# A two-layer graph network on one core: plain transfers grouped into fewer, larger ones

## The chip, the core and the metric

The kernel runs on one core of one Trainium2 chip. The core has a matrix engine (TensorE, PE in the profile; its weight loads are listed apart as PEld), VectorE (DVE), ScalarE (ACT), GpSimd (POOL) and SyncE (SP), and 16 DMA engines that move data between DRAM and the on-chip memory. SP does nothing but issue plain transfers; POOL computes a little and issues the indexed ones (a gather or a scatter whose row numbers come from a tile) and a few plain ones. The metric is the device time of one execution in microseconds.

## The reference

`x` is 2708 x 512 in float32, `adj` is 2708 x 2708 with a full diagonal and about 0.3% of the other entries set, to values between 0.05 and 1. Two layers follow each other, each with a residual and a layer norm:

```python
# layer 0
rowsum = adj.sum(axis=1)
d = jnp.where(rowsum > 0, rowsum ** (-0.5), 0.0)
g = relu(((d[:, None] * adj * d[None, :]) @ x) @ W + b)
x = layernorm(x + g)
# layer 1, 4 heads
y = x @ W_node + b_node
feats = jnp.einsum('nd,hdf->hnf', y, K)
s = leaky(einsum('hnf,hf->hn', feats, A_self) + einsum('hnf,hf->hn', feats, A_neigh))
attn = softmax(s[:, :, None] - 1e10 * (1.0 - adj)[None], axis=-1)
x = layernorm(x + relu(mean over h of (attn @ feats)))
```

In layer 1 the term with 1e10 leaves nothing of the softmax but a row's largest adj entry, so each row takes the features of one other row; and since the heads are averaged, `W_node` and the mean of `K` fold into one 512 x 512 matrix M (`m_sb`) with one bias row (`c_3`, `c_bc`).

## The kernel before

The 2708 rows are cut into 22 blocks of 128 rows (`NB`; the last has 20 rows, `NS` = 21 are full). All order is written by hand (`tc.manual_schedule()`): every engine and every queue works through its instructions in the order in which the program names them, and an instruction waits where it needs another engine's result or a buffer that is still in use. Pools with `bufs=n` give n buffers per name in turn; the writer of a buffer waits for the last reader of its previous content.

**Stage 1, to about 137 us.** For each block, SP loads its 1.35 MB of adj rows into one of nine slots (`a`, `load_blocks`, L289) and its rows of x (L525). PE turns x and multiplies it by W; ACT sums the adj rows (L296); POOL clears the diagonal (L307) and takes the root of the row sum (`root`, L262). `value` (L536) scales the product, giving v = d (x W), and stores it to `v_d` in DRAM: on POOL's queue for all but the last three blocks. DVE searches each adj row in three column thirds for its eight largest entries and their columns (`find`, L315). Blocks that the search has not reached by the end of stage 1 are searched later, between other work.

**Stage 2, to about 405 us.** A row has some eight neighbours. For each block, nine gathers fetch rows of `v_d` (`fetch_chunk`, L624, issued at L611): three "direct" ones (the first found column of each third), six from lists of what is left. The lists are made by `hot` (L385: for each third a `past` and a `hot` on DVE), `enlist` (a one-hot product on PE) and `listed` (L410, on DVE: `nth`, `one`, `own_f`, `sheet` and the lists). The fetched rows are summed by PE (`add_chunk`, L657 and L672, with small matrices that ACT or DVE forms) or by DVE (L662). Block `ib` also needs its own rows of v and of x: `load_own(ib + 2)` (L680, called at L1239) loads them two blocks ahead, on SP, into `vs` and `xr`. `norm_1` and the lines after it give h, the output of layer 0, in the tiles `h_early` (the first eight blocks) and `h_late`; each block of h is stored to `h_d` (L1188). Then `turn_h`, `u_product` and `u_store` (L772 to L798) give u = h M + c, stored to `u_e` (rows of the first `EARLY` = 18 blocks) or put by index into `u_d` (the rest). At L1232 to L1235 four stores, one for each of the blocks 9 to 12, fill the last block of `u_e` and `u_d` with finite values.

**Listed rows.** Rows that the search does not cover (over eight entries in a third, and the 20 rows of the last block) are listed once the search is done (`rank_1` to `rank_4`). Their rows of adj are gathered whole into `l_a` (`listed_a`, L981), and the full product with v is made: 22 turns (`listed_turn`) and 22 products (`listed_product`, L1008) on PE, against blocks of v that `listed_v` (L995) loads on SP into six buffers, `l_v`, six blocks ahead. When these steps come is written in `plan` (L1129), counted in blocks and chunks from the block at which the search ends.

**Stage 3, the output, from about 400 us.** For each block, `y_fetch` (L1042) gathers for each row the row of u of its largest neighbour, `y_1` (L1061) adds it to h, `root_1` and `root_2` (L739, L745) make the scale of the layer norm for a group of blocks, `y_3` applies it and the block is stored to `out`. The table `early_y` (L1073 to L1081) lays these steps out in pieces, in groups of three blocks. Rows whose largest neighbour is among the last blocks of u ("late" rows, at most four tiles) and the listed rows come last (L1256 to L1300) and are put into `out` by index; these puts wait for the plain stores of `out`. At the end a number from `bad` tells whether the sparse method covered the input; if not, a dense version runs instead (L1305), which it does not here.

Of the kernel before, what the change touches and what calls it, by code (L numbers as in the profile page):

```python
# [63 lines left out]
def tile_two_graph_layers(  # L64
# [36 lines left out]
    def store(dst, t, ib, queue=None):  # L101
        for lo, hi, r0 in parts(ib):
            (queue or nc.sync).dma_start(out=dst[r0 + lo : r0 + hi, :], in_=t[lo:hi])

    in_order = ExitStack()
# [279 lines left out]
    def hot(ib):  # L385

        lo = max(g for g in GROUPS if g <= ib)
        ends = starts[lo]
        h_t = search.tile([P, T, 2 * P], BF16, name="hot", bufs=2)
        for t in range(T):  # L390
            past = search.tile([P, 2 * P], BF16, name="past", bufs=2)
            nc.vector.tensor_scalar(past, slots, ends[:, 1, ib - lo, t : t + 1], None, op0=ALU.is_gt)  # L392
            nc.vector.scalar_tensor_tensor(  # L393
                h_t[:, t, :], slots, ends[:, 0, ib - lo, t : t + 1], past, op0=ALU.is_gt, op1=ALU.subtract
            )
        hots[ib] = h_t
# [13 lines left out]
    def listed(ib):  # L410

        ls = sheets.pop(ib)[:, : NL * W_REC].rearrange("p (n c) -> p n c", c=W_REC)
        nth = search.tile([P, NL], F32, name="nth", bufs=2)
        nc.vector.tensor_sub(nth, slot_no.rearrange("p t k -> p (t k)"), ls[:, :, 1])
        minus_row = search.tile([P, NL], F32, name="l_row", bufs=6)
        nc.vector.tensor_copy(minus_row, ls[:, :, 0])
        one = search.tile([P, NL, REST], F32, name="one", bufs=2)
        nc.vector.tensor_tensor(
# [5 lines left out]
        shape = [P, NL, 5, REST]  # L424
        own_f = search.tile(shape, F32, name="own_f", bufs=2)
        nc.vector.tensor_tensor(
# [4 lines left out]
        )  # L431
        t = search.tile([P, NL, 5], F32, name="sheet", bufs=2)
        nc.vector.tensor_reduce(t, own_f, axis=AX.X, op=ALU.add)
# [100 lines left out]
    pos_w = {}  # L534

    def value(i):  # L536

        pr = rows(i)
        vt = pool2.tile([P, D], F32, name=("vs", "xr")[i % 2], bufs=2)
        nc.scalar.activation(vt[:pr], pos_w.pop(i)[:pr], AF.Copy, scale=dinv[:pr, i : i + 1])  # L540
        store(v_d, vt, i, nc.gpsimd if i < NB - 3 else nc.sync)
        if i == 0:
            nc.gpsimd.dma_start(out=u_d[full - EARLY * P :, :], in_=vt[: N - full])
# [136 lines left out]
    def load_own(ib):  # L680
        if ib < NS:
            vs = pool2.tile([P, D], F32, name="vs", bufs=2)
            xr = pool2.tile([P, D], F32, name="xr", bufs=2)
            load(vs, v_d, ib)
            load(xr, x, ib)
            own[ib] = vs, xr

# [77 lines left out]
    def space(ib):  # L765
        if ib not in h_of:
            h_of[ib] = h_early[:, ib, :] if ib < NE else h_late[:, ib - NE, :]
        return h_of[ib]

    hTs = {}  # L770

# [5 lines left out]
    def u_product(ib):  # L777
        pr = P if ib == L else rows(ib)
        on_pe = searching[0]
        products_u[ib] = times(hTs.pop(ib), pr, m_sb, c_3 if on_pe else None), on_pe  # L780

    def u_store(ib):

        pr = P if ib == L else rows(ib)
        ut = dl["u"] if ib == L else pool2.tile([P, D], F32, name="ut", bufs=2)
        po, on_pe = products_u.pop(ib)
# [4 lines left out]
        if ib < EARLY - 1:  # L791
            store(u_e, ut, ib)
        elif ib == EARLY - 1:
            later(1, lambda: put(ut, u_e[:, :], dl["own"][:, ib : ib + 1], EARLY * P))
        elif ib != L:
            late_put = lambda: put(ut, u_d[:, :], dl["own_d"][:, ib : ib + 1], N - EARLY * P)
            late_put() if ib >= NS - 2 else later(3, late_put)
# [193 lines left out]
    def listed_root():  # L991
        dl["d"] = late.tile([P, 1], F32, name="l_d")
        root(dl["d"], dl["s2"])

    def listed_v(jb):  # L995
        if jb < NB:
            t = dl["v", jb] = late.tile([P, D], F32, name="l_v", bufs=6)
            load(t, v_d, jb)

# [8 lines left out]
    def listed_product(jb):  # L1008
# [5 lines left out]
        )  # L1014
        listed_v(jb + 6)
        if jb == NB - 1:
# [53 lines left out]

    GROUP = 3
    n_pieces = NS + 13
    early_y = [[] for _ in range(n_pieces)]  # L1073
    for n in range(NS):
        last = n // GROUP * GROUP + GROUP - 1
        early_y[n].append(lambda n=n: y_fetch(n))
        early_y[n + 6].append(lambda n=n: y_1(n))
        if n == last:
            early_y[last + 8].append(lambda n=n: root_1(n - GROUP + 1, n + 1))
            early_y[last + 9].append(lambda n=n: root_2(n - GROUP + 1, n + 1))  # L1080
        early_y[last + 10 + n % GROUP].append(lambda n=n: (y_3(n), store(out, h_of[n], n)))  # L1081

# [63 lines left out]
    for ib in range(NS):  # L1146
        pr = rows(ib)
        for c in range(C):
# [31 lines left out]
            if c == (2 if ib <= ROOTS_AT else 3) and ib:  # L1180
# [6 lines left out]
                norm_3(ib - 1, rows(ib - 1), space(ib - 1))  # L1187
                store(h_d, space(ib - 1), ib - 1)  # L1188
                waiting_h.append(ib - 1)
# [31 lines left out]
        if not finds and late is None:  # L1221
# [9 lines left out]
            nc.scalar.copy(c_bc, po)  # L1231
        at = ib - 10 + EARLY  # L1232
        if EARLY - 1 <= at < NS:

            store(*((u_e, space(ib - 9), at) if at < EARLY else (u_d, space(ib - 9), at - EARLY)))  # L1235
        if ib + 1 < NS:
# [12 lines left out]
    norm_v(ib, P, space(ib))  # L1249
    store(h_d, space(ib), ib)  # L1250
    stir(16)
# [44 lines left out]
    root_2(second[0], second[-1] + 1)  # L1296
    nc.vector.tensor_copy(bad_i, po[:1, :1])
    for n in second:
# [148 lines left out]
```

## Time and profile before

| | us |
|---|---|
| median of 3 runs | 490.34 (489.5 to 492.23) |
| profiled execution, its own time | 488.01 |
| its span in the trace | 486.3 |

Busy time by stretch of the span, in us, from the trace's table of time windows (PEclk is the granted clock of TensorE as a share of full speed, DMA the mean busy share of the 16 DMA engines):

| stretch (us) | length | PE | DVE | ACT | POOL | PEclk | DMA | GB/s |
|---|---|---|---|---|---|---|---|---|
| 0 to 115 | 115 | 90.99 | 95.07 | 94.35 | 49.72 | 0.93 | 1.01 | 367 |
| 115 to 137 | 22 | 21.02 | 18.67 | 19.18 | 11.20 | 0.98 | 0.54 | 200 |
| 137 to 270 | 133 | 113.20 | 128.49 | 84.55 | 100.11 | 0.97 | 0.81 | 256 |
| 270 to 310 | 40 | 29.57 | 31.18 | 22.89 | 28.60 | 0.88 | 0.91 | 311 |
| 310 to 400 | 90 | 88.82 | 65.81 | 48.33 | 65.70 | 0.98 | 0.92 | 323 |
| 400 to 414 | 14 | 13.59 | 10.66 | 4.50 | 8.02 | 1.00 | 0.80 | 258 |
| 414 to 486 | 72 | 19.64 | 41.85 | 38.51 | 41.99 | 0.68 | 0.63 | 208 |

The plain transfers that the change regroups, from the profile's list of DMA issues (number, KB of each, median us from issue to landing where the trace shows the landing): v stores on POOL's queue 10 `v_d<-vs` (7.3 us) and 9 `v_d<-xr` (7.5), `vs` 21 (4.9), `xr` 21 (5.9), `l_v` 21 (5.0), `u_e<-ut` 17, `h_d` 8 and 13 (3.6 and 2.9), `out_dram` 8 and 13 (4.8 and 4.4), all of 256 KB.

How to read the rest: a line of the timeline has a start in us, a duration in us, the engine (SPq and POOLq are issues on the queues of SP and POOL), the line of the code, the operation, and the tile written and the tiles read; in brackets stands the idle time before it and what ended that. Lines of the chain give shares of the span, followed back from the last instruction.

### The profile page before, as it was taken

The page shows a single profiled execution, that of the slowest core. Times are in us where ns is not written, and L with a number is a line of the kernel's source. Part 1 is how long each engine was busy: PE and PEld are TensorE (multiplying, and loading weights), DVE is VectorE, ACT ScalarE, POOL GpSimd, SP SyncE. Part 2 cuts the span into 40 slices and gives each one's busy share as a digit, 9 for nine tenths or more (in the row PEclk, how much of TensorE's full clock was granted, in tenths as well). Part 3 has the DMA queues.
Part 4 walks back from the last instruction along what each step waited for, and adds up shares of the span by engine and source line. Part 5 has one row for each costly group of instructions (what it writes and reads, how often), then busy time and mean ns, then how long its engine had stood idle before and what let it go on. Part 6 is the DMA issues. An engine that isn't in the chain of part 4 may idle for free.

```text
span 486.3 us, 5318 instructions
## 1 busy us (share of the span) xinstructions
PE 376.8 (77%) x1129; PEld 168.8 (35%) x1129; DVE 391.7 (81%) x1079; ACT 312.3 (64%) x575; POOL 305.3 (63%) x434
## 2 busy tenths in 40 slices
PE   4979788788978987799977958699999999880000
PEld 3434344333223333344323423344444444340000
DVE  2799989879799999999999996666667697667661
ACT  1599999797886556776773453865666322348680
POOL 2343544454477677777787577777777665677703
PEclk9998998798997999999999889799999999995555
DMA  7999999998548678889889789999999688469952
GB/s 232 419 398 416 422 339 371 357 336 342 197 119 286 202 235 264 263 253 315 272 258 290 228 261 371 376 325 376 369 367 313 219 270 269 138 194 308 322 193 84
DMA packets 51565, 140.67 MB, mean 289 GB/s; under 512 B 10617, under 2 KB 10617, under 8 KB 48688
## 3 DMA queue, kind: packets, MB, share of 16 engines
q0 software_dynamic: 21840, 68.29, 45.1%
q1 hardware_dynamic: 29684, 71.95, 39.4%
q8 instruction: 11, 0.18, 0.2%
q14 instruction: 30, 0.25, 0.2%
HBM read 117.33 MB, written 24.99 MB: 293 GB/s over the span
## 4 chain that ended last, share of the span: by engine, by line
DVE 28%; PE 19%; DMA 7%; issue 5%; ACT 3%; POOL 3%; POOLq 0%; DVEq 0%; ACTq 0%
PE acc L672 7%; PE po L235 6%; PE acc_l L1012 4%; DVE ats L319 4%; DVE vals L318 3%; DVE hot L393 3%; DVE vs L662 2%; DMA l_a<-in_adj_dram,to_read 2%; DMA g<-u_e,idx 2%; POOL g L611 1%; DVE past L392 1%; DVE h_early L712 1%; DMA g<-v_d,l_col 1%; DVE h_late L1063 1%; DVE vs L711 1%
## 5 line engine op out<-in xcount | busy, mean ns | idle before, releaser
L611 POOL DMA_INDIRECT g<-v_d,l_col x126 | 127.3, 1010 | 42.6 <-issue 22.1
L672 PE MATMUL acc<-g,s 128*128 128x512 f32 x278 | 143.2, 628 | 4.3 <-DMA g<-v_d,l_col 2.6
L235 PE MATMUL acc<-w_sb,sT 128*128 128x512 f32 (+1 forms) x176 | 89.1, 654 | 0.0
L235 PE MATMUL po<-m_sb,sT 128*128 128x512 f32 x176 | 80.8, 603 | 2.7 <-ACT sT L226 2.7
L611 POOL DMA_INDIRECT g<-v_d,cols x63 | 63.4, 1007 | 19.7 <-issue 13.1
L318 DVE MAX8 vals<-a 128x8 f32<-128x896 f32 (+2 forms) x66 | 71.7, 1087 | 2.8 <-ACT a L299 2.8
L319 DVE FIND_INDEX8 ats<-vals,a 128x8 uint32<-128x896 f32 (+2 forms) x66 | 72.1, 1092 | 0.0
L672 PEld LDWEIGHTS acc<-g,s 128*128 128x128 f32 x278 | 49.1, 196 | 50.1 <-issue 42.3
L305 ACT ACTIVATE a<-a 128x2708 f32<-128x2708 f32 (+1 forms) x22 | 54.4, 2471 | 12.4 <-DVE ats L319 12.4
L299 ACT ACTIVATE a<-a 128x2708 f32<-128x2708 f32 (+1 forms) x22 | 54.8, 2490 | 10.0 <-POOL a L311 10.0
L235 PEld LDWEIGHTS po<-m_sb,sT 128*128 128x128 f32 x176 | 33.5, 194 | 45.0 <-issue 38.2
L235 PEld LDWEIGHTS acc<-w_sb,sT 128*128 128x128 f32 (+1 forms) x176 | 34.7, 208 | 38.6 <-issue 38.5
L649 ACT ACTIVATE s<-s,l_val,l_minus 128x128 f32<-128x128 f32 x86 | 42.4, 493 | 2.9
L311 POOL TENSOR_SCALAR_AFFINE_SELECT a<-a 128x128 f32<-128x128 f32 (+1 forms) x22 | 7.2, 327 | 56.0 <-DMA a<-in_adj_dram 49.7
L226 ACT COPY sT<-tp 128x512 f32<-128x512 f32 (+1 forms) x44 | 25.8, 586 | 24.8 <-PE tp L224 24.8
L662 DVE SCALAR_TENSOR_TENSOR vs<-g,scaled,vs 128x512 f32<-128x512 f32 x50 | 37.2, 744 | 0.1
L224 PE MATMUL tp<-ident,x 128*128 128x128 f32 (+1 forms) x88 | 15.4, 303 | 23.6 <-DMA x<-in_x_dram 15.5
L648 ACT ACTIVATE s<-place,l_row 128x128 f32<-128x128 f32 x86 | 33.4, 388 | 0.0
L393 DVE SCALAR_TENSOR_TENSOR hot<-slots,ends,past 128x256 bf16<-128x256 bf16 x63 | 30.6, 485 | 2.2
L1052 POOL DMA_INDIRECT g<-u_e,idx x21 | 21.9, 1041 | 7.1 <-issue 5.5
L726 ACT ACTIVATE nms<-tot 128x1 f32<-128x1 f32 x10 | 2.0, 202 | 34.8 <-DVE h_early L712 19.5
L721 ACT ACTIVATE xr<-h_late,nms 128x512 f32<-128x512 f32 x11 | 7.9, 722 | 24.7 <-DVE nms L720 24.7
(265 smaller groups left out, 579.5 us busy)
## 6 DMA issues: line engine op xcount, KB each, us to landing
a<-in_adj_dram SPq DMA_DIRECT2D x21, 1354.0 KB, 9.3
x<-in_x_dram SPq DMA_DIRECT2D x21, 256.0 KB, 19.1
vs<-v_d SPq DMA_DIRECT2D x21, 256.0 KB, 4.9
xr<-in_x_dram SPq DMA_DIRECT2D x21, 256.0 KB, 5.9
l_v<-v_d SPq DMA_DIRECT2D x21, 256.0 KB, 5.0
u_e<-ut SPq DMA_DIRECT2D x17, 256.0 KB
h_d<-h_late SPq DMA_DIRECT2D x13, 256.0 KB, 2.9
out_dram<-h_late SPq DMA_DIRECT2D x13, 256.0 KB, 4.4
```

Source lines behind the costliest of these rows:

```text
L226: copy(sT[:, :, :pr], ps[:, :, :pr])
L235: nc.tensor.matmul(po[:pr], sT[:, f, :pr], wt[:, f, :], start=(f == 0 and row_3 is None), stop=(f == ND - 1))
L299: nc.scalar.activation(a, a, AF.Copy, accum_out=sums[:pr, ib : ib + 1])
L305: nc.scalar.activation(a, a, AF.Relu, scale=-1.0, accum_out=bad[:pr, NB + ib : NB + ib + 1])
L318: nc.vector.max(out=vals[:pr, ib, t, :], in_=part)
L319: nc.vector.max_index(out=ats[:pr, ib, t, :], in_max=vals[:pr, ib, t, :], in_values=part)
L393: nc.vector.scalar_tensor_tensor(h_t[:, t, :], slots, ends[:, 0, ib - lo, t : t + 1], past, op0=ALU.is_gt, op1=ALU.subtract)
L611: nc.gpsimd.indirect_dma_start(out=t[:pr], out_offset=None, in_=src, in_offset=bass.IndirectOffsetOnAxis(ap=ap, axis=0))
L648: nc.scalar.activation(s[:, :pr], place[:, :pr], AF.Abs, bias=minus_row[:, t : t + 1])
L649: nc.scalar.activation(s[:, :pr], s[:, :pr], AF.Relu, scale=minus_val[:, t : t + 1], bias=val[:, t : t + 1])
L662: nc.vector.scalar_tensor_tensor(vs, g, scaled[:, ib, CHUNKS[c][1], 0:1], vs, op0=ALU.mult, op1=ALU.add)
L672: nc.tensor.matmul(acc[ib][:pr], ss.pop((ib, c))[:k, :pr], g[:k], start=(first and not bias_on_pe(ib)), stop=(c == len(CHUNKS) - 1),)
```

## The change

Plain transfers of one block each become transfers of several blocks, through one helper, `many`, that views consecutive row blocks of a DRAM tensor as one 128-row pattern. Stores of v go by pairs of blocks, except the last four blocks, which go as before; own rows of v and x come by pairs, loaded at even blocks (so the pair for blocks ib+2 and ib+3 comes where block ib+2 alone came); u is stored by pairs; h is stored in groups that end at `H_ENDS`; the v blocks of the listed product come by three, in two buffers of three instead of six of one; output blocks are normalised and stored in groups that end at `ENDS`, eight groups of two or three instead of seven of three. The four fills go out together after block 11 as two transfers. `past`, `nth`, `one`, `own_f` and `sheet` have one buffer instead of two. `bad_i` is written by a comparison instead of a copy.

```diff
             (queue or nc.sync).dma_start(out=dst[r0 + lo : r0 + hi, :], in_=t[lo:hi])
+    def many(dram_t, lo, hi):
+        return dram_t[lo * P : hi * P, :].rearrange("(n p) d -> p n d", p=P)
...
         h_t = search.tile([P, T, 2 * P], BF16, name="hot", bufs=2)
         for t in range(T):
-            past = search.tile([P, 2 * P], BF16, name="past", bufs=2)
+            past = search.tile([P, 2 * P], BF16, name="past", bufs=1)
             nc.vector.tensor_scalar(past, slots, ends[:, 1, ib - lo, t : t + 1], None, op0=ALU.is_gt)
...
         ls = sheets.pop(ib)[:, : NL * W_REC].rearrange("p (n c) -> p n c", c=W_REC)
-        nth = search.tile([P, NL], F32, name="nth", bufs=2)
+        nth = search.tile([P, NL], F32, name="nth", bufs=1)
         nc.vector.tensor_sub(nth, slot_no.rearrange("p t k -> p (t k)"), ls[:, :, 1])
         minus_row = search.tile([P, NL], F32, name="l_row", bufs=6)
         nc.vector.tensor_copy(minus_row, ls[:, :, 0])
-        one = search.tile([P, NL, REST], F32, name="one", bufs=2)
+        one = search.tile([P, NL, REST], F32, name="one", bufs=1)
         nc.vector.tensor_tensor(
...
         )
         shape = [P, NL, 5, REST]
-        own_f = search.tile(shape, F32, name="own_f", bufs=2)
+        own_f = search.tile(shape, F32, name="own_f", bufs=1)
         nc.vector.tensor_tensor(
...
             op=ALU.mult,
         )
-        t = search.tile([P, NL, 5], F32, name="sheet", bufs=2)
+        t = search.tile([P, NL, 5], F32, name="sheet", bufs=1)
         nc.vector.tensor_reduce(t, own_f, axis=AX.X, op=ALU.add)
...
     pos_w = {}
+    v_pair = []
...
         pr = rows(i)
-        vt = pool2.tile([P, D], F32, name=("vs", "xr")[i % 2], bufs=2)
+        if not i % 2:
+            v_pair[:] = [pool2.tile([P, 2, D], F32, name=("vs", "xr")[i // 2 % 2], bufs=2)]
+        vt = v_pair[0][:, i % 2, :]
         nc.scalar.activation(vt[:pr], pos_w.pop(i)[:pr], AF.Copy, scale=dinv[:pr, i : i + 1])
-        store(v_d, vt, i, nc.gpsimd if i < NB - 3 else nc.sync)
+        if i >= NB - 4:
+            store(v_d, vt, i, nc.gpsimd if i < NB - 3 else nc.sync)
+        elif i % 2:
+            nc.gpsimd.dma_start(out=many(v_d, i - 1, i + 1), in_=v_pair[0])
         if i == 0:
...
     def load_own(ib):
-        if ib < NS:
-            vs = pool2.tile([P, D], F32, name="vs", bufs=2)
-            xr = pool2.tile([P, D], F32, name="xr", bufs=2)
-            load(vs, v_d, ib)
-            load(xr, x, ib)
-            own[ib] = vs, xr
+        if ib < NS and not ib % 2:
+            hi = min(ib + 2, NS)
+            vs = pool2.tile([P, 2, D], F32, name="vs", bufs=2)
+            xr = pool2.tile([P, 2, D], F32, name="xr", bufs=2)
+            nc.sync.dma_start(out=vs[:, : hi - ib], in_=many(v_d, ib, hi))
+            nc.sync.dma_start(out=xr[:, : hi - ib], in_=many(x, ib, hi))
+            for k in range(ib, hi):
+                own[k] = vs[:, k - ib, :], xr[:, k - ib, :]
...
         return h_of[ib]
+    H_ENDS = [4, NE, 12, 16, 19, 20, NS]
+    def h_part(lo, hi):
+        return h_early[:, lo:hi, :] if hi <= NE else h_late[:, lo - NE : hi - NE, :]
+    def store_h(done):
+        if done in H_ENDS:
+            lo = ([0] + H_ENDS)[H_ENDS.index(done)]
+            nc.sync.dma_start(out=many(h_d, lo, done), in_=h_part(lo, done))
...
         products_u[ib] = times(hTs.pop(ib), pr, m_sb, c_3 if on_pe else None), on_pe
+    u_pair = []
...
         pr = P if ib == L else rows(ib)
-        ut = dl["u"] if ib == L else pool2.tile([P, D], F32, name="ut", bufs=2)
+        if ib == L:
+            ut = dl["u"]
+        else:
+            if not ib % 2:
+                u_pair[:] = [pool2.tile([P, 2, D], F32, name="ut", bufs=2)]
+            ut = u_pair[0][:, ib % 2, :]
         po, on_pe = products_u.pop(ib)
...
             nc.vector.tensor_add(ut[:pr], po[:pr], c_bc[:pr])
         if ib < EARLY - 1:
-            store(u_e, ut, ib)
+            if ib % 2 or ib == EARLY - 2:
+                lo = ib - ib % 2
+                nc.sync.dma_start(out=many(u_e, lo, ib + 1), in_=u_pair[0][:, : ib + 1 - lo])
         elif ib == EARLY - 1:
...
         root(dl["d"], dl["s2"])
+    L_V = 3
     def listed_v(jb):
-        if jb < NB:
-            t = dl["v", jb] = late.tile([P, D], F32, name="l_v", bufs=6)
-            load(t, v_d, jb)
+        if jb < NB and not jb % L_V:
+            t = late.tile([P, L_V, D], F32, name="l_v", bufs=2)
+            hi = min(jb + L_V, NS)
+            if hi > jb:
+                nc.sync.dma_start(out=t[:, : hi - jb], in_=many(v_d, jb, hi))
+            if jb + L_V > NS:
+                load(t[:, NS - jb, :], v_d, NS)
+            for k in range(jb, min(jb + L_V, NB)):
+                dl["v", k] = t[:, k - jb, :]
...
             dl["acc"], dl.pop(("t", jb))[:kr], dl.pop(("v", jb))[:kr], start=(jb == 0), stop=(jb == NB - 1)
         )
-        listed_v(jb + 6)
+        if jb % L_V == L_V - 1:
+            listed_v(jb + 1 + L_V)
         if jb == NB - 1:
...
-    GROUP = 3
+    ENDS = [3, 6, NE, 11, 14, 17, 19, NS]
     n_pieces = NS + 13
     early_y = [[] for _ in range(n_pieces)]
-    for n in range(NS):
-        last = n // GROUP * GROUP + GROUP - 1
-        early_y[n].append(lambda n=n: y_fetch(n))
-        early_y[n + 6].append(lambda n=n: y_1(n))
-        if n == last:
-            early_y[last + 8].append(lambda n=n: root_1(n - GROUP + 1, n + 1))
-            early_y[last + 9].append(lambda n=n: root_2(n - GROUP + 1, n + 1))
-        early_y[last + 10 + n % GROUP].append(lambda n=n: (y_3(n), store(out, h_of[n], n)))
+    def out_store(lo, hi):
+        nc.sync.dma_start(out=many(out, lo, hi), in_=h_part(lo, hi))
+    lo = 0
+    for hi in ENDS:
+        for n in range(lo, hi):
+            early_y[n].append(lambda n=n: y_fetch(n))
+            early_y[n + 6].append(lambda n=n: y_1(n))
+        early_y[hi + 7].append(lambda lo=lo, hi=hi: root_1(lo, hi))
+        early_y[hi + 8].append(lambda lo=lo, hi=hi: root_2(lo, hi))
+        for n in range(lo, hi):
+            early_y[hi + 9 + n - lo].append(lambda n=n: y_3(n))
+        early_y[hi + 8 + hi - lo].append(lambda lo=lo, hi=hi: out_store(lo, hi))
+        lo = hi
...
                     nc.scalar.activation(nbs[:, k], nms[:, k], AF.Copy, scale=rss[:, k])
                 norm_3(ib - 1, rows(ib - 1), space(ib - 1))
-                store(h_d, space(ib - 1), ib - 1)
+                space(ib - 1)
+                store_h(ib)
                 waiting_h.append(ib - 1)
...
             nc.tensor.matmul(po, every[:T], c_3, start=True, stop=True)
             nc.scalar.copy(c_bc, po)
-        at = ib - 10 + EARLY
-        if EARLY - 1 <= at < NS:
-            store(*((u_e, space(ib - 9), at) if at < EARLY else (u_d, space(ib - 9), at - EARLY)))
+        if ib == 11:
+            nc.sync.dma_start(out=many(u_e, EARLY - 1, EARLY), in_=h_part(0, 1))
+            nc.sync.dma_start(out=many(u_d, 0, NS - EARLY), in_=h_part(1, 1 + NS - EARLY))
         if ib + 1 < NS:
...
     root_2(ib, ib + 1)
     norm_v(ib, P, space(ib))
-    store(h_d, space(ib), ib)
+    store_h(NS)
     stir(16)
...
         rows_out(n)
     root_2(second[0], second[-1] + 1)
-    nc.vector.tensor_copy(bad_i, po[:1, :1])
+    nc.vector.tensor_scalar(bad_i, po[:1, :1], 0.0, None, op0=ALU.is_gt)
     for n in second:
```

## The prediction

> **What bounds the kernel now.** I read the page first (busy shares, the chain that ended last), then the table of time windows, then the timelines of the stretches in which something waits, and last the waits.
>
> ```profile
> span 486.3 us, 5318 instructions
> PE 376.8 (77%) x1129; PEld 168.8 (35%) x1129; DVE 391.7 (81%) x1079; ACT 312.3 (64%) x575; POOL 305.3 (63%) x434
> DVE 28%; PE 19%; DMA 7%; issue 5%; ACT 3%; POOL 3%; POOLq 0%; DVEq 0%; ACTq 0%
> ...
> 165.00:200.00 35.00, 27.77 (x88) 11.60 (x87) 33.91 (x83) 24.24 (x51) 25.79 (x27) 1.00 0.79 241
> 225.00:251.00 26.00, 24.83 (x73) 9.71 (x72) 25.27 (x63) 16.85 (x34) 20.72 (x21) 1.00 0.84 274
> 290.00:305.00 15.00, 12.27 (x38) 5.32 (x36) 9.59 (x31) 6.40 (x11) 10.49 (x12) 1.00 1.00 370
> 320.00:380.00 60.00, 60.00 (x197) 28.16 (x195) 39.69 (x121) 35.81 (x96) 46.27 (x46) 1.00 0.98 349
> 450.00:470.00 20.00, 0.19 (x2) 0.12 (x2) 12.37 (x54) 13.62 (x32) 9.83 (x10) 0.50 0.81 284
> ```
>
> The window rows give busy us of PE, PEld, DVE, ACT and POOL, then the granted clock, the DMA share and GB/s. The bound changes by stage. From 137 to 270 it is DVE (33.91 of 35, 25.27 of 26); from 310 to 380 PE (60.00 of 60); after 414 a chain of POOL fetches, DVE, ACT. Around 300 all engines stand still, for one fetch: the listed rows of adj, `l_a`.
>
> ```profile
> 83.02 0.48 DVE L393 SCALAR_TENSOR_TENSOR hot<-slots,ends,past 128x256 bf16<-128x256 bf16 x1
> 83.42 0.28 DVE L392 TENSOR_SCALAR past<-slots,ends 128x256 bf16<-128x256 bf16 x1
> 83.74 0.48 DVE L393 SCALAR_TENSOR_TENSOR hot<-slots,ends,past 128x256 bf16<-128x256 bf16 x1
> ...
> 288.42 3.12 SPq L99 DMA_DIRECT2D l_v<-v_d  x6
> 294.92 0.32 SPq L103 DMA_DIRECT2D u_e<-ut  x1
> 296.92 0.32 SPq L99 DMA_DIRECT2D vs<-v_d  x1
> ...
> 291.82 1.09 POOL L611 DMA_INDIRECT l_a<-in_adj_dram,to_read  x1 [0.31 <-DMA g<-v_d,l_col]
> 302.83 2.46 ACT L989 ACTIVATE l_a<-l_a 128x2708 f32<-128x2708 f32 x1 [3.27 <-DMA l_a<-in_adj_dram,to_read]
> 309.00:312.00 3.00, 3.00 (x8) 1.52 (x9) 2.96 (x6) 2.90 (x9) 2.22 (x6) 0.50 1.01 386
> ...
> 457.05 0.69 DVE L1063 SCALAR_TENSOR_TENSOR h_late<-g,h_late 128x512 f32<-128x512 f32 x1 [2.41 <-DMA g<-u_e,idx]
> 473.80 1.02 POOL L1029 DMA_INDIRECT out_dram<-g,to_put  x1 [11.23 <-ACT g L756]
> ```
>
> A start, a duration, the instruction and what ended its wait. `l_a` (1.39 MB) takes 11.0 us from issue to landing, beside six `l_v` loads; ACT stands idle 3.27 us for it, PE has gaps of 3.2 and 2.4 us, and then works at half clock until 313.8. No line among the waits of DVE, PE or ACT names `vs`, `xr`, `u_e`, `h_d` or `l_v` as what it waited for, apart from 1.2 us in five pieces on PE's weight load before `l_v` products.
>
> **The change, part by part.** The built order of instructions tells the moves.
>
> *Bytes and issues.* The bytes stay: 71.95 MB on SP's queue and 68.29 on POOL's. SP issues 118 transfers instead of 189. SP's own time (0.32 us each) is hidden, since no engine waits for SP's issue; a grouped issue has the 0.38 us of the 128x4x512 weights as nearest row.
>
> *v by pairs (POOL).* 19 stores become 10, at 0.65 us each for 128 descriptors and 1.34 for the 512 of K: a pair by interpolation 0.88, so POOL saves 9 x (2 x 0.65 - 0.88) = 3.8 us. POOL waits 49.7 us for `a` there, so 0. Moved later by one block: half the v bytes; behind them in POOL's queue stand the diagonal and the row-sum root of the next block, which on even blocks no longer wait. The last four blocks are stored as before, so the first fetch (138.75) keeps its time. DMA is full there (1.05), so I give +-1 us: a pair is 0.7 us at 350 GB/s.
>
> *One buffer for `past` (DVE).* The second and third `past` of each `hot` now wait on DVE's own semaphore for the `hot` that reads the buffer: 42 such waits in the built order, where there were none. In the rows above, an instruction without a wait starts 0.40 us after a `hot` of 0.48 (it overlaps by 0.08); one with such a wait (`hot` behind `past`) starts 0.04 after the end. So each costs 0.12 us. From 137 to 270, where DVE is the bound, `hot` runs 10 times (30 L393: 6, 9, 6, 6, 3 in the windows), 20 waits, **+2.4 us**; behind them on DVE stand the searches, and POOL's root at 271.88 waits for DVE, then the gathers up to `l_a`. The other 22 lie beside PE's bound or POOL's queue, but for one `hot` at 389.8 on the chain (+0.2). Bounds 0 and +2.6. `nth`, `one`, `own_f` and `sheet` with one buffer are reused a block later: 0.
> [...]
>
> *`vs`, `xr`, `u`, `h`, `l_v` on SP, and `l_a`.* In order on SP, the grouped queue lets `l_v` (1.57 MB) and `vs`/`xr` of blocks 12, 13 (1.05) go out behind the `u` pair of 281.8 instead of behind the `h_d` store of 288.05. SP's transfers issued from 281.8 until `l_a` landed were 3.93 MB (u_e 2, fill 2, vs/xr 4, h_d 1, l_v 6, at 0.262); now 3.15 (pair, `l_v`, one `vs`/`xr` pair), all by 286: the next, a `u` pair, waits for the `u` of 311.4, and the fills and `h_d` stand behind it. The DMAs are full from 284 on, so 0.78 MB less at 370 GB/s (the window's) lets `l_a` land **2.1 us** earlier. Bounds: 0 (the early burst only delays the gathers ahead of `l_a` in POOL's ring) and 3.3 (ACT's idle time; more is hidden by ACT's own work). A loss I exclude: less is queued in front of `l_a`. Next late is the ACT chain to the h block that PE transposes (2.4 us).
>
> *Half clock.* From 309 to 313.8 PE works 4.8 us for what takes 2.4 at full clock. With the idle time 2.1 us shorter the drop may fail to come or last one step less: I take half, **-1.2**, bounds 0 and -2.4.
> [...]
>
> *`l_v` by three with two buffers, 310 to 380.* A refill goes out after products 2, 5, 8... and is needed 9 chunks later: 13.1 us (the u products of the chain recur every 13.14). One of 256 KB lands in 5.0, at worst 14.2 us in the burst of 288. A 786 KB one, at 175 GB/s (half of 349), takes 2 x 262/175 = 3.0 us more: 8. Covered by 5 us: 0; if the cover goes, PE loses what is over 13.1, five times.
>
> *`h` by four, fills, outputs, after 405.* The `h` store at 412 is three blocks, 0.52 MB more beside the two puts into `u_e`: 1.5 us of DMA in a stretch with a share of 0.43, I take +0.3. Outputs leave as 8 stores; the fetch that landed after 6.0 us (451 to 457) meets 0.5 MB less, -1.0 towards the median 4.6. The norm groups are 8 instead of 7: one more round DVE, ACT, DVE after 457, 0.9 wait and 0.9 work, of which 0.6 beside ACT's squares, +1.2. The last store carries 512 KB: 0.7 us more at 370 GB/s; its order is one piece earlier, but ACT reaches it no sooner: +0.5, as the puts wait for it. Together **+1.0**, bounds -1.0 and +2.5. `bad_i` as a comparison instead of a cast: one DVE instruction either way.
>
> **Sum**: +2.4 +0.2 -2.1 -1.2 +1.0 = +0.3 us against the profiled execution's 488.01, which is 2.3 under the median of 490.34. **490.6 us**, no change.
>
> **The rivals.** (a) Faster: `l_a` lands before ACT is free and the clock stays up: -3.3 -2.4 +2.6 +1.0 = -2.1, and without the cost of the `past` waits -4.7: 488.2 to 485.6. For it: SP's queue is silent from 286 to 311. Against it: the gathers ahead of `l_a` share the same ring.
> (b) Slower: `l_a` lands no earlier, since the burst of 3.15 MB is still draining when `l_a` starts. Then +2.6 +1.0 = +3.6, **493.9**. It decides from a saving under 1.1 us on `l_a` with the clock still dropping. For it: POOL's gathers ask 210 GB/s (262 KB per 1.25 us) of some 350 already. Against it: the count of bytes.
> (c) Slower: `l_v` refills land late on PE. At 15 us instead of 13.1, five times 1.9: 490.6 + 9.5 = 500. The 14.2 us row speaks for it; that every refill finds SP free, against.
> (d) All of it hidden, waits included: 490.3, inside the forecast.
>
> **How the numbers follow.** Forecast with (d) 0.40, (a) 0.25, (b) 0.25, (c) 0.10. What a measurement can tell from no change is about 0.5%, 2.45 us. So faster 0.25, same 0.40, slower 0.35. The range leaves out the lower end of (a) with the bound -1 of the v pairs, and (c): 486.0 to 495.5. The likeliest case's own range is 487.9 to 492.8.
>
> **What would show it.** Right: `past` behind `hot` starts 0.52 us after it, not 0.40; the first six `l_v` blocks issued near 283; `l_a` to landing near 9 us, ACT's wait near 1; no wait of PE on `l_v`; a last output store that lands just before the first put. Wrong: DVE's stretch from 137 to 270 as long as before, or shortened by something that I cost at nothing, such as the v stores; PE idle before `l_v` products; a different clock pattern in the first 115 us.

## The result and the profile after

The changed kernel took 493.57 us (median of 13 runs, 489.87 to 496.71) and the kernel before 489.59 in as many (488.47 to 492.23): a ratio of 1.008, with a 95% interval of 1.0059 to 1.0101. It is slower by 4 us. The profiled execution took 492.36 us against 488.01, with spans of 490.7 and 486.3. The experiments further down ran on three chips on which the kernel before took 532 us, and their ratios leave out executions over 1.5% above the fastest of the same kernel; this section is about the first pair of traces only.

From the page of the changed kernel: span, busy shares, and two of the DMA queues.

```profile
span 490.7 us, 5118 instructions
PE 375.9 (77%) x1129; PEld 167.9 (34%) x1129; DVE 398.7 (81%) x1085; ACT 312.4 (64%) x576; POOL 301.8 (62%) x425
...
q0 software_dynamic: 21696, 68.29, 43.8%
q1 hardware_dynamic: 28548, 71.95, 39.4%
```

PE, ACT and the bytes are as before (376.8 and 312.3 us; 68.29 and 71.95 MB). DVE has 7.0 us more busy time (398.7 against 391.7). The chain of this trace breaks off at the last put, so the time is followed in another way: most instructions of DVE, ACT and POOL stand in the same order in both programs, and the start of one and the same instruction can be compared. Where the difference grows, time was lost.

| instruction | before | after | difference |
|---|---|---|---|
| DVE, copy to `ends`, end of stage 1 | 130.07 | 129.71 | -0.36 |
| DVE, second `past` of a block in the DVE-bound stretch | 259.30 | 263.43 | +4.13 |
| DVE, third `past` of the last block ahead of `l_a` | 291.05 | 295.83 | +4.78 |
| ACT, sum of `l_a` | 302.83 | 305.12 | +2.29 |
| DVE, `ut` of the block behind it | 322.00 | 324.12 | +2.12 |
| POOL, first put into `u_e` | 409.13 | 411.94 | +2.81 |
| POOL, first fetch of the output stage | 417.74 | 421.95 | +4.21 |
| POOL, first put into `out` | 473.80 | 478.21 | +4.41 |
| end of the span | 486.3 | 490.7 | +4.4 |

**The loss from 130 to 291 is in `past`.** Groups of DVE instructions by shape from 137 to 270, first of before, then of after; the columns behind the bar are busy us, mean ns of one, and idle us ahead of them.

```profile
L393 DVE SCALAR_TENSOR_TENSOR hot<-slots,ends,past 128x256 bf16<-128x256 bf16 x30 | 14.5, 485 | 1.1
L392 DVE TENSOR_SCALAR past<-slots,ends 128x256 bf16<-128x256 bf16 x30 | 8.3, 278 | 0.0
```

```profile
L397 DVE SCALAR_TENSOR_TENSOR hot<-slots,ends,past 128x256 bf16<-128x256 bf16 x30 | 14.7, 490 | 1.1
L396 DVE TENSOR_SCALAR past<-slots,ends 128x256 bf16<-128x256 bf16 x30 | 9.8, 328 | 0.7
```

The three `past` and three `hot` of a block took 2.23 us before (first start to last end, mean of the ten blocks between 137 and 275) and take 2.63 after: 10 x 0.40 = 4.0 us. Part of it is the wait that was forecast: a `past` starts 0.52 us after a `hot`, not 0.40, twice in a block, so 0.24 of the 0.40. The rest is in `past` itself, and this timeline of the changed kernel shows where (start, duration, instruction; DVE and POOL together):

```profile
198.59 0.28 DVE L396 TENSOR_SCALAR past<-slots,ends 128x256 bf16<-128x256 bf16 x1
198.90 0.50 DVE L397 SCALAR_TENSOR_TENSOR hot<-slots,ends,past 128x256 bf16<-128x256 bf16 x1
198.94 0.96 POOL L622 DMA_INDIRECT g<-v_d,cols  x1 [0.30 <-issue]
199.44 0.51 DVE L396 TENSOR_SCALAR past<-slots,ends 128x256 bf16<-128x256 bf16 x1
199.98 0.48 DVE L397 SCALAR_TENSOR_TENSOR hot<-slots,ends,past 128x256 bf16<-128x256 bf16 x1
200.21 1.09 POOL L622 DMA_INDIRECT g<-v_d,l_col  x1 [0.30 <-issue]
200.50 0.29 DVE L396 TENSOR_SCALAR past<-slots,ends 128x256 bf16<-128x256 bf16 x1
```

The second `past` starts 0.50 us into a gather that POOL issues (198.94 to 199.90), and lasts not 0.28 but 0.51 us, to 0.05 after the gather's end. This is no single case. Of the 63 `past` of this trace, all 15 that begin 0.49 to 0.66 us after a gather's start end 0.03 to 0.06 us after that gather does, and take 0.34 to 0.51 us; those that begin earlier or later in a gather take 0.27 to 0.30. Before, only two of 63 began in that part of a gather, and just those two were long (0.51 and 0.46). The self-wait moves the second and third `past` by 0.12 and 0.24 us, and so into it.

Why such a `past` lasts until the gather's end no run shows. A gather on POOL at the same time is not enough for it: the fourteen `past` of this trace that begin 0.29 to 0.40 us into a gather take 0.27 to 0.29 us. Some gathers are longer too: of the thirteen from `v_d` that have a `past` begin 0.29 to 0.40 us into them, twelve take 1.08 to 1.19 us, like the second gather above, while 103 of the 150 in which no `past` begins take 0.94 to 0.96. Whether the `past` or the `hot` ahead of it goes with that is not shown.

DVE's lateness reaches POOL behind that stretch: POOL's root of 271.88 waits there for ACT, which waits for `h_late` from DVE. It starts at 276.01 in the changed kernel (+4.13), and the idle time ahead of it is 5.54 us, it was 3.04.

**What `l_a` gives back.** The changed kernel's gather and sum of `l_a`, from the timelines of POOL and ACT:

```profile
295.53 1.09 POOL L622 DMA_INDIRECT l_a<-in_adj_dram,to_read  x1 [0.30 <-DVE past L396]
...
305.12 2.46 ACT L1023 ACTIVATE l_a<-l_a 128x2708 f32<-128x2708 f32 x1 [0.95 <-DMA l_a<-in_adj_dram,to_read]
```

ACT's wait is 0.95 us, it was 3.27; from issue to use it is 9.59 us, it was 11.01. POOL is 3.71 us late at the issue, ACT 2.29 at the use.

**The half clock comes later and lasts half as long.** Windows of the changed kernel (busy us of PE, PEld, DVE, ACT and POOL, granted clock, DMA share, GB/s):

```profile
306.00:308.00 2.00, 1.41 (x5) 0.47 (x4) 0.00 (x0) 1.98 (x3) 1.39 (x3) 1.00 1.03 385
308.00:310.00 2.00, 0.91 (x3) 0.08 (x1) 0.58 (x5) 1.96 (x4) 1.54 (x2) 1.00 0.84 275
310.00:312.00 2.00, 0.66 (x4) 0.42 (x4) 1.85 (x6) 1.93 (x6) 1.55 (x2) 1.00 0.77 238
312.00:314.00 2.00, 1.74 (x3) 0.77 (x4) 1.97 (x4) 1.93 (x7) 1.83 (x4) 0.56 0.70 188
314.00:316.00 2.00, 2.00 (x10) 0.94 (x9) 1.89 (x5) 0.49 (x2) 1.42 (x3) 0.59 0.83 313
316.00:318.00 2.00, 2.00 (x8) 0.99 (x7) 1.90 (x8) 1.84 (x5) 1.39 (x3) 1.00 1.02 364
```

The same for the kernel before:

```profile
306.00:308.00 2.00, 0.63 (x2) 0.00 (x0) 0.84 (x5) 1.96 (x5) 1.63 (x2) 0.72 1.04 414
308.00:310.00 2.00, 1.00 (x5) 0.75 (x6) 1.93 (x5) 1.93 (x6) 1.61 (x4) 0.50 1.05 406
310.00:312.00 2.00, 2.00 (x5) 0.78 (x5) 2.00 (x4) 1.93 (x6) 1.30 (x4) 0.50 0.99 380
312.00:314.00 2.00, 2.00 (x11) 1.00 (x10) 1.76 (x6) 0.36 (x3) 1.70 (x2) 0.57 0.92 334
```

A mean clock of 0.56 over 2 us is 1.76 us at half; with the next row (0.59) the changed kernel has 3.4 us. The four rows of before hold 6.8 us. In steps of 0.2 us the clock is 0.50 in every one from 312.4 to 315.6 in the changed kernel, and in every one from 307.0 to 313.6 before.

**The output stage starts 1.4 us later still.** POOL at the turn to the output stage, first two lines of before, then the changed kernel:

```profile
414.19 0.99 POOL L1029 DMA_INDIRECT u_e<-ut,put_own  x1 [4.04 <-DMA h_d<-h_late]
417.74 1.05 POOL L1052 DMA_INDIRECT g<-u_e,idx  x1 [1.00 <-DMA u_e<-ut,put_own]
```

```profile
411.94 1.03 POOL L1072 DMA_INDIRECT u_e<-l_u,to_put  x1 [0.30 <-DVE ut L822]
415.94 0.99 POOL L1072 DMA_INDIRECT u_e<-ut,put_own  x1 [2.97 <-DVE vs L713]
417.23 0.99 POOL L1072 DMA_INDIRECT u_d<-l_u,put_d  x1 [0.30 <-issue]
421.95 1.05 POOL L1095 DMA_INDIRECT g<-u_e,idx  x1 [3.73 <-PE po L239]
```

From the second put to the fetch it is 6.01 us, before 3.55; from the first put to the second 4.00, before 5.06, where the second put waited 4.04 us for a store of h. The bracket of the changed kernel's fetch names PE, but in all fourteen traces of this case the fetch starts 0.81 us after the last completion signal of the second put. Before, the put's sixteen signals come from 416.69 to 416.94. In the changed kernel fifteen come by 419.06, and the last 2.1 us later, at 421.14. The DMA view of the changed kernel from the second put to 421.2 (busy tenths in 40 slices; packets, MB and share of the queue; us from the put's issue to its landing):

```profile
DMA  9898989989898929999900563000000000000000
q8 instruction: 1, 0.02, 2.1%
u_e<-ut,put_own POOLq DMA_INDIRECT x1, 5.2
```

One packet of 16 KB of queue q8, whose kind the page gives as "instruction", starts at 416.04 and takes 1.75 us. In the trace of before no packet of q8 starts between the put and its landing (one of 8 KB of the other such queue, q14, does, for 0.34 us), and the put lands in 2.7 us. The traces of the experiments show below that this goes together. From that fetch to the first put into `out` the two kernels differ by 0.2 us, eight groups or seven.

### The profile page after: what moved, and what is told of

It reads as the page before. It is cut to its first block, busy times and chain, and to the rows that moved or that the text cites. A ratio compares the mean times of both kernels' runs of the same rounds, so it can differ in the third digit from the quotient of the medians.

```text
span 490.7 us, 5118 instructions
## 1 busy us (share of the span) xinstructions
PE 375.9 (77%) x1129; PEld 167.9 (34%) x1129; DVE 398.7 (81%) x1085; ACT 312.4 (64%) x576; POOL 301.8 (62%) x425
## 3 DMA queue, kind: packets, MB, share of 16 engines
q0 software_dynamic: 21696, 68.29, 43.8%
q1 hardware_dynamic: 28548, 71.95, 39.4%
## 5 line engine op out<-in xcount | busy, mean ns | idle before, releaser
L239 PE MATMUL po<-m_sb,sT 128*128 128x512 f32 x176 | 82.4, 614 | 5.1 <-ACT sT L230 5.1
L239 PE MATMUL acc<-w_sb,sT 128*128 128x512 f32 (+1 forms) x176 | 83.9, 622 | 0.0
L622 POOL DMA_INDIRECT g<-v_d,cols x63 | 64.7, 1027 | 19.7 <-issue 12.8
L239 PEld LDWEIGHTS acc<-w_sb,sT 128*128 128x128 f32 (+1 forms) x176 | 32.9, 198 | 35.1 <-issue 35.0
L228 PEld LDWEIGHTS tp<-ident,x 128*128 128x128 f32 (+1 forms) x88 | 10.1, 147 | 40.2 <-ACT sT L230 19.9
```

The costliest lines, as they stand in the source:

```text
L239: nc.tensor.matmul(po[:pr], sT[:, f, :pr], wt[:, f, :], start=(f == 0 and row_3 is None), stop=(f == ND - 1))
L622: nc.gpsimd.indirect_dma_start(out=t[:pr], out_offset=None, in_=src, in_offset=bass.IndirectOffsetOnAxis(ap=ap, axis=0))
```

## The experiments

On the three chips of these runs (e on one, f on another, g and h on the third) the kernel before took 532 to 533 us (7 to 30 runs). Whether the chip makes the difference to the 490 us of the first pair is not shown. The trace of the kernel before there (run h1, below) shows why 1% is hard to tell: engines stand still for want of something that the profile does not show (PE, DVE and ACT together for 25.0 us). The ratios expected below were worked out from the first pair, and the changed kernel itself has 0.990 here (run g1), not 1.008. So each run is read in two ways: its ratio to the kernel before on the same chip, and the local durations in its trace, which those stretches do not touch.

### Two buffers for `past`

```diff
-            past = search.tile([P, 2 * P], BF16, name="past", bufs=1)
+            past = search.tile([P, 2 * P], BF16, name="past", bufs=2)
...
-        return search.tile([P, NB], F32, name="col", bufs=8)
+        return search.tile([P, NB], F32, name="col", bufs=7)
```

(The second edit makes room for the second buffer.)

> The changed kernel with two buffers for past again (col has 7 buffers instead of 8 to make room), all grouped transfers kept. Theory 1 (the self-waits of past cost 4.0 us between 137 and 270, and all of it but what l_a's landing takes back rides to the end): l_a is issued near 291.8 again and lands 9.6 us later, at 301.4, instead of 305.1; the time falls by 3.7 us against the changed kernel, to 489.9, a ratio of 1.000 to 1.002 to the kernel before. Rival (the slack ahead of l_a absorbs what DVE saves, the loss lies in the grouped transfers): under 1 us of gain, 492.6 or more, ratio above 1.006.

> The first run of this kernel fell on a chip on which the kernel before took 532 us instead of 490, with stretches of 10 us in which all engines stood still; it is looked at again. Two buffers for past, grouped transfers kept. Theory 1 (self-waits of past): 3.7 us faster than the changed kernel, ratio to the kernel before 1.000 to 1.002, past 0.28 us long and 0.40 after hot throughout. Rival (the loss lies in the grouped transfers): ratio above 1.006.

Its control, with the edit of `col` alone, ran beside a third run of it:

> The control for the run with two buffers for past: the changed kernel with one buffer for past, but col with 7 buffers, so that against the next run only past differs. Theory 1: like the changed kernel, 493.6, ratio to before 1.006 to 1.010 where the kernel before takes 490; on a chip where it takes 530, where PE and the others stand still for up to 10 us at a time, no more than 1% can be told.

> The same kernel with two buffers for past (otherwise as the control beside it, on the same chip). Theory 1 (the self-waits ride to the end): 3 to 4.4 us less than the control. Rival (the wait for l_a or another stall behind takes back what DVE saves): less than 1 us below the control, although hot takes 2.24 instead of 2.6 us for a block.

And the reverse, one buffer for `past` in the kernel before (`bufs=2` to `bufs=1` at L391, nothing else), twice:

> The kernel before with one buffer for past and nothing else. Theory 1: DVE is 4.0 us late at 270 (20 waits at 0.12 us and the past instructions that start about 0.5 us into a gather's work on POOL and then last 0.45 to 0.51 us instead of 0.28), l_a is issued that much later and lands 11 us after, nothing takes it back: +3.7 to +4.2, 493.6, ratio 1.008. Rival (the idle 3.3 us of ACT ahead of l_a absorbs it): +0.7, 490.3, ratio 1.0015.

> The kernel before with one buffer for past and nothing else, looked at again for the same reason. Theory 1: DVE 4.0 us late at 270, nothing takes it back, +3.7 to +4.2 us, ratio 1.008. Rival (ACT's idle 3.3 us ahead of l_a absorbs it): +0.7, ratio 1.0015.

Measured, with the mean time of the six instructions of a block over the whole trace (21 blocks):

| run | `past` buffers | six instructions of a block, us | ratio to before |
|---|---|---|---|
| first trace, before | 2 | 2.25 | |
| first trace, after | 1 | 2.61 | 1.008 (1.0059 to 1.0101) |
| e1, changed, two buffers | 2 | 2.27 | 0.976 (0.967 to 0.985) |
| f1, the same | 2 | 2.27 | 0.990 (0.983 to 0.997) |
| g2, the same | 2 | 2.28 | 0.9915 (0.987 to 0.996) |
| g1, changed, `col` alone | 1 | 2.57 | 0.990 (0.984 to 0.996) |
| e2, before, one buffer | 1 | 2.55 | 0.997 (0.992 to 1.002) |
| f2, the same | 1 | 2.59 | 1.0105 (1.001 to 1.020) |

The groups of DVE in the whole trace of g1 (one buffer), then of f1 (two):

```profile
L397 DVE SCALAR_TENSOR_TENSOR hot<-slots,ends,past 128x256 bf16<-128x256 bf16 x63 | 30.6, 486 | 2.5 <-DVE past L396 0.3
L396 DVE TENSOR_SCALAR past<-slots,ends 128x256 bf16<-128x256 bf16 x63 | 19.2, 305 | 1.6
```

```profile
L397 DVE SCALAR_TENSOR_TENSOR hot<-slots,ends,past 128x256 bf16<-128x256 bf16 x63 | 30.6, 486 | 2.2
L396 DVE TENSOR_SCALAR past<-slots,ends 128x256 bf16<-128x256 bf16 x63 | 18.3, 291 | 0.0
```

What follows: the local cost is shown, in both kernels and both ways: one buffer costs 0.3 us a block, with 1.6 us of idle time where there was none. A part of it can come without the single buffer: f4 (below), with two, has 2.38, and six of its `past` begin 0.49 to 0.66 us into a gather and last 0.35 to 0.50 us. That the cost rides to the end is not shown here. On the same chip g1 and g2 differ by 0.0015 in the ratio, 0.8 us and the wrong way round, inside intervals of 0.4 to 0.6% to either side, where 3 us or more were expected. e1 (beside e3 and e4, with one buffer on its chip) and f2 point the expected way, e2 does not, and f1 has the 0.990 that g1 has with one buffer. For the first pair of traces the claim rests on the table of starts and on the wait by which POOL takes over DVE's lateness. Two buffers for `past` in the changed kernel were not run on a chip where the kernel before takes 490 us.

### The `h` stores at the turn to the output stage

```diff
-    H_ENDS = [4, NE, 12, 16, 19, 20, NS]
+    H_ENDS = [4, NE, 12, 16, 17, 18, 19, 20, NS]
```

> The changed kernel with the h stores of blocks 16, 17 and 18 issued one by one, instead of three blocks in one transfer at 414.8. Theory 1 (that burst of 0.79 MB holds up the put into u_e issued at 415.9, which the first fetch of the output stage waits for: 6.0 us from issue to that fetch instead of 3.6): the fetch starts 1.4 to 2.4 us earlier, 491.2 to 492.2, ratio to before near 1.004. Rival (the put is late for another reason, the three-block store is hidden): no change, 493.6, ratio 1.008.

> The changed kernel with two buffers for past, and the h stores of blocks 16, 17 and 18 one by one. Against the run with two buffers for past alone this tells the h burst apart. Theory 1 (the three-block store of h holds up the put into u_e before the output stage): a further 1.4 to 2.4 us, ratio to before 0.996 to 0.998. Rival (that store is hidden): the same as with two buffers alone, 1.000 to 1.002.

Measured: e3 0.991 (0.987 to 0.995), f3 0.999 (0.993 to 1.004). f3 is no faster than f1 on its chip (0.990, with the three-block store), and e3 has no such partner on its own; so no gain in the whole. The traces tell more. All fourteen, by the store of h ahead of the second put and by whether a 16 KB packet of the instruction queue q8 starts between that put and its landing (us from the second put, the last column from the first; some traces lack a part of the sixteen signals, and the recorded ones are taken):

| traces | blocks in the `h` store | 16 KB packet of q8, us | last signal but one | last signal | fetch | fetch, from the first put |
|---|---|---|---|---|---|---|
| before, e2, f2, f4, h1, h2 | 1 | none | 2.67 to 2.72 | 2.71 to 2.75 | 3.52 to 3.56 | 8.06 to 9.13 |
| e3, f3 | 1 | 1.55, 1.23 | 2.73, 2.75 | 4.30, 3.88 | 5.11, 4.69 | 9.50, 9.06 |
| e1 | 3 | none | 3.18 | 3.21 | 4.02 | 7.97 |
| after, e4, f1, g1, g2 | 3 | 0.94 to 1.75 | 3.13 to 3.37 | 4.60 to 5.20 | 5.41 to 6.01 | 9.38 to 10.01 |

So the three-block store costs 0.4 to 0.7 us, on all parts of the put, and theory 1 of e3 and f3 asked too much of it. The rest, 1.1 to 2.1 us on the put's last part, comes in just the seven traces with such a packet in between. The store of h shows the same in the changed kernel's first trace: fifteen signals by 418.32, the last at 420.51. That the packet holds up one of the sixteen parts is an inference from these fourteen traces: no run moved the packet, and the trace does not say which DMA engine took it.

### The outputs

The table of output steps and the single stores as before (`GROUP = 3`, one store per block), all else changed:

```diff
-    ENDS = [3, 6, NE, 11, 14, 17, 19, NS]
+    GROUP = 3
...
-        early_y[hi + 8 + hi - lo].append(lambda lo=lo, hi=hi: out_store(lo, hi))
+        early_y[last + 10 + n % GROUP].append(lambda n=n: (y_3(n), store(out, h_of[n], n)))
```

> The changed kernel with the output steps as before: seven groups of three blocks, 21 stores of one block. Theory 1 (between the first fetch of the output stage and the end the two kernels differ by 0.2 us, the extra round of the eighth group is hidden by late fetches): 493.4, within 0.5 us of the changed kernel, ratio to before 1.007 to 1.009. Rival (the prediction's term, the eighth group and the larger last store cost 1.7 us and fewer bytes in the way of fetches give back 1): 0.7 to 1.7 us faster than the changed kernel, 492 to 492.9, ratio 1.005 to 1.0065.

Measured: 0.994 (0.989 to 0.999), beside 0.990 of g1 on another chip: no gain from going back, within what these chips can tell. With the 0.2 us of the first pair of traces, the grouped output is about neutral.

### u, h and the fills alone

The kernel before with `u_pair`, `H_ENDS` (blocks 16 to 20 one by one) and the two fill transfers of the change, and nothing else of it.

```diff
-                store(h_d, space(ib - 1), ib - 1)
+                space(ib - 1)
+                store_h(ib)
...
-            store(u_e, ut, ib)
+            if ib % 2 or ib == EARLY - 2:
+                lo = ib - ib % 2
+                nc.sync.dma_start(out=many(u_e, lo, ib + 1), in_=u_pair[0][:, : ib + 1 - lo])
...
-        at = ib - 10 + EARLY
-        if EARLY - 1 <= at < NS:
+        if ib == 11:
```

> The kernel before with only these parts of the change: u stored by pairs, h by four (blocks 16 to 20 one by one), the four fills as two transfers after block 11; v, vs, xr, l_v, the outputs and all buffers of the search as before. This takes 0.78 MB out of the queue ahead of l_a and lets l_v go out early, and nothing else of the change. Theory 1 (l_a lands about 2 us earlier for it: 9.0 to 9.6 us from issue instead of 11.0): 1.4 to 2.1 us faster than before, ratio 0.996 to 0.997. Rival (in the changed kernel l_a landed sooner after its issue only because it was issued later, when less was in flight): no gain, ratio 0.999 to 1.001.

Measured: 1.0003 (0.9947 to 1.006): no gain in the whole, though the interval holds both theories. Locally, `l_a` goes from issue to ACT's use in 9.61 us; in h1 (the kernel before) it took 10.84, in h2 11.00 and in the first trace 11.01, while all eight traces with the SP order of the change up to there have 9.38 to 9.88. That supports the account of the bytes in the queue. It does not settle it: f2, with the old order, has 9.70, and e2 11.60 of which ACT idled 2.0.

### The other half, and the kernel before in a trace of its own

v by pairs, own rows by pairs and `l_v` by three in the kernel before:

```diff
-        if ib < NS:
-            vs = pool2.tile([P, D], F32, name="vs", bufs=2)
+        if ib < NS and not ib % 2:
+            hi = min(ib + 2, NS)
+            vs = pool2.tile([P, 2, D], F32, name="vs", bufs=2)
...
-            t = dl["v", jb] = late.tile([P, D], F32, name="l_v", bufs=6)
+            t = late.tile([P, L_V, D], F32, name="l_v", bufs=2)
```

> The kernel before with the other half of the grouped transfers: v stored by pairs, own rows of v and x loaded by pairs, l_v by three in two buffers; past, u, h, the fills and the outputs as before. On the chips of the runs up to now the whole change had 0.990, and u, h and the fills alone 1.000. Theory 1 (the 1% on those chips comes from these three): ratio 0.988 to 0.994 there, and on a chip with 490 us 0.997 to 1.001, since nothing waited for these transfers. Rival (it comes from the outputs or from all of it together): 0.997 to 1.003 on either.

> The kernel before with 7 buffers for col instead of 8, for its trace: on the chips of the runs up to now the kernel before took 532 to 533 us and no trace of it was taken there. Time: as the kernel before, ratio 0.997 to 1.003. Theory 1 (on those chips engines stand still for want of something that no line of this program holds back, and that hides a difference of 4 us on DVE): PE, ACT and DVE idle together for 15 to 25 us in stretches over 1 us, against 5.9 us in the first trace of the kernel before, and hot takes 2.23 us for a block. Where the kernel before takes 490 here, those stretches are near 6 us. Rival (the longer time is slower transfers): mean time of a gather from issue to landing well above 5.1 us and no more common idle time than before.

Measured, with four runs each: h2 0.994 (0.986 to 1.003), h1 0.996 (0.987 to 1.006). The two theories on h2 cannot be told apart. h1, which is the kernel before but for a spare buffer, lies 0.4% from 1: an error of that size is to be expected in the other ratios too. The page of h1 (span, chain by engine) and two lines of its groups:

```profile
span 524.2 us, 5318 instructions
...
PE 32%; DVE 11%; issue 10%; ACT 5%; DMA 3%; POOL 3%; another core or an unknown queue 3%; POOLq 0%; DVEq 0%
...
L226 ACT COPY sT<-tp 128x512 f32<-128x512 f32 (+1 forms) x44 | 25.4, 578 | 44.4 <-remote 17.7
L790 DVE TENSOR_TENSOR ut<-po,c_bc 128x512 f32<-128x512 f32 x15 | 10.3, 688 | 22.2 <-remote 10.7
```

Against the first trace of before, DVE's share of the chain falls from 28% to 11%, and "issue", time in which the engine waited for nothing that the profile shows, rises from 5% to 10%, with 3% more from an unknown queue. PE, DVE and ACT are idle together for 25.0 us in stretches over 1 us (up to their last instruction), against 5.4; the longest is 12.5 us, where ACT waits from 454.98 on for a copy whose operand PE had finished near 459:

```profile
454.68 0.30 ACT L742 ACTIVATE sds<-sqs,eps 128x1 f32<-128x1 f32 x1
472.64 0.59 ACT L226 COPY sT<-tp 128x512 f32<-128x512 f32 x1 [17.66 <-remote]
```

POOL goes on with its fetches meanwhile (from 460 to 473 it is busy for 9.94 of 13 us, at a DMA share of 0.67), so it is neither the chip nor the DMA as a whole. Busy times are near those of the first trace (DVE 392.3 us against 391.7, PE 382.3 against 376.8). So the first theory holds in its first half, that the engines stand still; that a 4 us difference on DVE therefore has less weight, where DVE is 11% of the chain, is argued and not shown. The rival, slower transfers, is not tested: this trace has the landings of too few gathers. What the engines wait for stays open.

## Why the prediction was right or wrong

It said 490.6 us, 486.0 to 495.5, most likely no change. The time, 493.57, lies in the range. By the prediction's own measure (0.5%) the 0.8% is slower, to which 0.35 was given, and it lies outside the 487.9 to 492.8 of the likeliest case. It comes close to the 493.9 of rival (b), but not by (b)'s mechanism: `l_a` did land earlier. The sum was +0.3 us, and the traces show +4.4; that the range holds the time all the same is the room left in it for (b), and so in part luck. The terms of the sum against the table of starts:

| term | forecast, us | shown, us |
|---|---|---|
| v by pairs | 0 (-1 to +1) | -0.4 |
| `past`, 130 to 291 | +2.4 (0 to +2.6) | +5.1, of it 4.0 in ten blocks' `past` and `hot` |
| `l_a` | -2.1 (0 to -3.3) | -2.5 |
| half clock | -1.2 (0 to -2.4) | -0.2 |
| `l_v` by three; `hot` at 389.8 | +0.2 | +0.7 |
| `h` store at the turn | +0.3 | +1.4 |
| outputs | +0.7 | +0.2 |
| sum | +0.3 | +4.4 |

- **`past`: the mechanism right, the size not.** The waits are there, cost 0.12 us each as forecast, and reach POOL and `l_a` by the path that was named. The term was taken per wait, and left out what a moved instruction runs into: the second price, up to 0.22 us for a `past` that begins half way through a gather. The upper bound of +2.6 was therefore no bound. The trace of before had the rows for it: a `past` of 0.51 us at 291.05 and one of 0.46 at 309.12, each beside a gather.
- **`l_a`: right.** ACT's wait was forecast near 1 and is 0.95, issue to landing near 9 and is 9.59. 1.4 us of the 2.5 is the faster landing; the rest is that POOL came to the issue 3.7 us late and not 4.8. The `l_v` loads went out at 286.4 and not near 283, as late as the `u` pair that they stand behind (285.95 for 281.82).
- **Half clock: the step shown, the gain not.** It lasts 3.4 us instead of 6.8, one step less, as taken (the drops of the two traces, but for the one at the end of each, last 3.4 or 6.8 us); but between the sum of `l_a` and the `ut` of the block behind it the difference moves by 0.2 us, not by 1.2. The 1.2 was the author's estimate, half of the 2.4 us by which PE was slower there, and no run shows it. What else stood on that path is not shown.
- **The `h` store: its price about right, a term missing.** The store costs 0.4 to 0.7 us on the put behind it, for a forecast of 0.3. The sum left out two things: the second put no longer waits for a store of h, which gives back 1.1 us, and the put's last part lands 2.1 us after the others, beside the 16 KB packet of the instruction queue q8. In the table above, +1.4 is the sum of these.
- **v by pairs: a slip without effect.** A pair of 0.52 MB takes 1.5 us at 350 GB/s (an estimate, from the 349 of the window of 320 to 380); the 0.7 us behind the bound is one block's. The stretch shows -0.4.
- **Cover of `l_v`: right.** PE's weight loads wait 0.9 us in all for `l_v`; before it was 1.2. Rival (c) did not come.
- **The chances.** Bounds of terms were taken from the nearest rows, but several lay one-sided in the same direction: all three misses (`past`, the half clock, the turn to the output stage) made the kernel slower.

## What to carry to other kernels

Room for larger transfers has a price where it is taken from: a second buffer of a 0.3 us helper on the engine that bounds a stage was worth 4 us of that stage in the first pair of traces, more than the grouped transfers were seen to give. When an engine is moved by a tenth of a microsecond, look at what it then coincides with, not at the wait alone. Grouping transfers that nobody waits for gained nothing here that could be measured; the one gain in sight, 1.4 us on the transfer that everybody waited for, goes with the new order on SP's queue, which is not settled. Where a wait is put down to an engine, look at the completion signals of the transfers too: of the sixteen of the second put in the changed kernel's first trace, fifteen came by 419.06 and the last at 421.14.

## What the runs showed that was not expected

- **`past` and POOL's gathers.** In the first pair of traces a `past` of 128 x 256 that begins 0.49 to 0.66 us after a gather of about 0.95 us is issued lasts until 0.03 to 0.06 us after its end (17 of 17); at other phases it takes 0.27 to 0.30 us.
- **A packet of an instruction queue and the last part of a transfer.** Seven of the fourteen traces have a 16 KB packet of queue q8 (0.94 to 1.75 us) starting between the second put and its landing, and in just these the put's last signal comes 1.1 to 2.1 us after the others.
- **The verdict is not the same everywhere.** Where the kernel before takes 490 us, the change is 0.8% slower; on a chip where it takes 532, the changed kernel (with one spare buffer less, run g1) is 1.0% faster, 0.984 to 0.996. There the engines wait for something unseen (run h1: PE, DVE and ACT idle together for 25.0 us, against 5.4), and DVE is 11% of the chain, not 28%. Which part of the change gains there is not settled: u, h and the fills alone have 1.000, the other loads 0.994, the changed kernel with the old outputs 0.994. No version was found that beats both kernels on both.
